# A four-layer graph network: the hidden pass's softmax inverses spread by DMA instead of matmul, and an adjacency asked for ahead

## The chip, the cores and the metric

The kernel runs on one NeuronCore of a Trainium2 chip. The metric is the device time of one execution in microseconds (us), lower is better; times are medians over runs. Five engines with instruction queues of their own share the work: PE (matmuls), DVE (vector), ACT (scalar), POOL (GpSimd) and SP, which here only issues transfers (DMAs). ACT and POOL issue transfers too. PSUM is the memory of eight banks that matmuls write into.

## The reference

Four layers on a graph of n = 3327 nodes with 256 features each. Every layer is `x = layernorm(x + gnn(x, adj))`.

```python
# layer 0: pairwise scores through all 256 features
score = einsum('ijc,c->ij', leaky_relu(g_src[:, None] + g_tgt[None]), a_w)   # masked by adj
y0 = softmax(score) @ g_tgt
# layer 1 (and 2, without leaky_relu): scores are a sum of two numbers
e = leaky_relu(s1[:, None] + s2[None, :]);  e = where(adj == 0, -1e9, e)
y1 = softmax(e) @ (h @ W.T)
# layer 3: two passes of four heads with 64 features each
h = einsum('nf,hfd->hnd', x, W)
e = leaky_relu(f1[:, :, None] + f2[:, None, :], 0.2)                          # masked by adj
out = elu(einsum('hnm,hmd->hnd', softmax(e), h))                              # heads side by side
```

Layer 3 applies its pass twice, the second time on the output of the first. In layers 1 and 3 exp(leaky_relu(a + b)) is a maximum of two products, so that one entry of the weight matrix is a `max` and a `mult` (by the adjacency). The sum over a row of weights is carried along as one more column, and the division by it comes at the end.

## The kernel before, in words

The nodes form 26 tiles of 128 rows (the last has 127). Columns of the result are worked in four **blocks** of 7, 7, 6 and 6 tiles, 896 or 768 columns wide.

Layer 0 (`sparse0`) gathers neighbours' rows by indirect DMAs on POOL. On its way it already makes layer 1's features of tiles 0 to 19 and stores them in DRAM (`feats_d`). The last six tiles are normalised and projected after layer 0, by generators that run beside layer 1's first block: `last_group` reads their sums back (`take`, DMAs of ACT), yields four times, takes the statistics (`settle`) and normalises; then `prepare` turns and projects them.

Layers 1 to 3 are in `layers`. `one_head` does layers 1 and 2, `many_heads` the two passes of layer 3 (`l3a`, `l3b`). Both loop over blocks, and within a block over the 26 tiles j of neighbours. In layer 1 `adjacent` loads the int32 adjacency tile `at_i` (SP), casts it to bf16 (`at`, ACT, L1638) and stores it to `at_d` for the later layers, which load it from there. `weigh` (L1621, DVE) makes the weights `e` from `rate`, a feature column and the adjacency. PE multiplies them with the features: L1705 in `one_head`; in `many_heads` L1752 for the features (eight groups of 32 rows, two halves of the columns) and L1760 for the sums of the weights.

`e` and `at_i` share one ring of eight buffers, the tag "e" of the pool `edges`. In layer 3 one j needs four `e` tiles, one for each head. In that ring the kernel also puts `sums`, the copy of the sums of a finished block.

The order in which the engines take up work is mostly the order in which the program is written (`manual_schedule`): on PE all through, on DVE and ACT in layer 3 and in layer 1's first block. `in_order` also holds POOL and SP to it, and is closed at the end of that block. Elsewhere a scheduler places the instructions.

Side work is done by generators in the list `pending`: `work_off` takes one step of them after the matmuls of j=0 and of every j from 4 on, one yield being one step. Thus the finishing of a block of layer 3 runs beside the next block. `finish_hidden` does that for `l3a`. It takes `inverses` (L1795: for each tile a matmul of `sums` with `heads_at` turns the sums over to partitions, and DVE takes reciprocals). Then it works on units of two tiles in stages, each so many steps after the first (`staged`, lags 0, 3, 6, 7): `spread` multiplies each inverse column, broadcast to 64 columns, with the identity (L1834), so that every partition has its row of inverses, and ACT copies the result; `scale` multiplies `o` by it and starts the elu (`below`, two ACT instructions); `elu` ends it; `project` (L1549) makes the second pass's features. `send_rates` and `load_rates` pass the second pass's rates through DRAM. `finish_last` does the same for `l3b`, with `inverses`, transposes back (L1883), the elu, the residual and the norm (`add`).

The tag "spread" of the pool `work` has four buffers, for `spreads`, `both`, `rate_rows` and others.

Of the kernel before, what the change touches and what calls it, by code (L numbers as in the profile page):

```python
# [50 lines left out]
def gat_stack(  # L51
# [59 lines left out]
    feats_d = dram.tile([EARLY * P, dim + 2], F32, name="feats_d")  # L111

# [157 lines left out]
    def sparse0(lost):  # L270
        GROUP, TURNS, LEAD, SPREAD = 4, 22, 8, 8
        starts = [sum(SETS[:s]) for s in range(len(SETS))]
        with ExitStack() as s0:
# [1028 lines left out]
            def last_group():  # L1302
                s = len(SETS) - 1
                take(s)
                for _ in range(4):
                    yield
# [191 lines left out]
    def layers(rs, early=0, rest=None):  # L1498
# [127 lines left out]

        def adjacent(j, b, first=False):
# [8 lines left out]
            at_i = edges.tile([P, wide], I32, tag="e", name="at_i", bufs=8)  # L1636
            copy_rows(nc.sync, at_i[:pn, :w], adj_t[j * P : j * P + pn, c0:c1])
# [51 lines left out]
        def one_head(layer, nxt, banks_next):  # L1689

            for b, block in enumerate(blocks):
                work_until(lambda: not layer.leaky or layer.rate[b] is not None)
                accs = [bank(s) for s in range(len(block))]
                for j in range(nt):
# [17 lines left out]
                    if layer is l1 and b == 0:  # L1712
                        work_off(2 if j > 10 else 1)
                        fetch([j + 3])
                        if j > early and late:
                            l1.load_rates(late.pop(0))
                    elif j >= LATER:
                        work_off()
# [10 lines left out]
                if b == 0:  # L1729
                    nxt = nxt()  # L1730
                pending.append(prepare(nxt, b, banks_next, normed=False))

        def many_heads(layer, nxt, finish):

            pairs = layer.nh // 2
            for b, block in enumerate(blocks):
# [34 lines left out]
                sums = edges.tile([P, wide], F32, tag="e", name="sums", bufs=8)  # L1771
# [3 lines left out]
                for x, (lo, hi) in enumerate(parts):  # L1775
                    nc.scalar.copy(sums[:, lo:hi], accs[x][pairs][:, : hi - lo])
# [12 lines left out]
        def inverses(block, sums, inv):  # L1789
# [3 lines left out]
            for s, it in enumerate(block):  # L1793
                pn = rows_of(it)
                nc.tensor.matmul(  # L1795
                    turned[:pn, s * heads : (s + 1) * heads], sums[:, s * P : s * P + pn], heads_at,
                    start=True, stop=True,
# [16 lines left out]
        def finish_hidden(b, o, sums):  # L1814
            block = blocks[b]
            inv = small.tile([P, max(sizes) * heads], F32, tag="invs", name="invs", bufs=2)
            yield from inverses(block, sums, inv)
            held = {}

            def cols(u):  # L1820
                return u[0] * P, min((u[-1] + 1) * P, cols_of(block)[1] - cols_of(block)[0])

            def spread(u):

                lo, hi = cols(u)
                m = misc((6, 7))
                m = m.rearrange("p (x i) -> p x i", x=heads // 2)
                for s in u:
                    pn = rows_of(block[s])
                    at0 = s * P - lo  # L1830
                    for h_of in range(heads):
                        p, q = divmod(h_of, 2)
                        k = s * heads + h_of
                        nc.tensor.matmul(  # L1834
# [262 lines left out]
```

## Time and profile before

| | |
|---|---|
| median of 3 runs | 2979.46 us (2978.26 to 2981.44) |
| the profiled execution's own time | 2983.31 us |
| its span in the profile | 2981.5 us |
| mean granted PE clock | 0.871 |
| busy: PE, DVE, ACT, POOL | 79%, 72%, 28%, 33% of the span |
| layer 0 | 0 to about 1363 us |
| layer 1, first block | about 1363 to 1465 us |
| `l3a` and `l3b` | about 1975 to 2981 us |

The table is read with the strip of 40 slices (each 74.5 us; a digit is the busy share in tenths): the stages have different bounds, and a share over the whole span says little about one of them. The stages' times are from the timeline. A group line of the profile has the line of the kernel, the engine, the operation, what it writes and reads, and the shapes; a line of the timeline begins with its start and its length in us, and ends with how many instructions it merges and with the idle time before them.

### The profile page before, as it was taken

The page shows a single profiled execution, that of the slowest core. Times are in us where ns is not written, and L with a number is a line of the kernel's source. Part 1 is how long each engine was busy: PE and PEld are TensorE (multiplying, and loading weights), DVE is VectorE, ACT ScalarE, POOL GpSimd, SP SyncE. Part 2 cuts the span into 40 slices and gives each one's busy share as a digit, 9 for nine tenths or more (in the row PEclk, how much of TensorE's full clock was granted, in tenths as well). Part 3 has the DMA queues.
Part 4 walks back from the last instruction along what each step waited for, and adds up shares of the span by engine and source line. Part 5 has one row for each costly group of instructions (what it writes and reads, how often), then busy time and mean ns, then how long its engine had stood idle before and what let it go on. Part 6 is the DMA issues. An engine that isn't in the chain of part 4 may idle for free.

```text
span 2981.5 us, 45479 instructions
## 1 busy us (share of the span) xinstructions
PE 2345.0 (79%) x16101; PEld 1308.0 (44%) x16122; DVE 2141.0 (72%) x5633; ACT 846.6 (28%) x2372; POOL 992.6 (33%) x1061
## 2 busy tenths in 40 slices
PE   7566757556554506557999999999999999999997
PEld 4222323222221203225888888853444554534332
DVE  6789799968876437764455421158989889899997
ACT  3244445443343304443344311101011110110111
POOL 2676767777777777770000000000000000000000
PEclk8577778777677758888999999999999999999998
DMA  7785665545544345446766533321221221212211
GB/s 234 202 262 144 186 170 161 143 134 160 156 115 110 107 112 145 132 123 188 240 199 199 164 94 106 105 85 47 69 72 44 73 66 51 69 45 62 56 46 47
DMA packets 178607, 366.95 MB, mean 123 GB/s; under 512 B 34140, under 2 KB 119467, under 8 KB 177348
## 3 DMA queue, kind: packets, MB, share of 16 engines
q1 hardware_dynamic: 103994, 178.49, 21.3%
q0 software_dynamic: 51008, 155.70, 19.2%
q10 hardware_dynamic: 23370, 29.76, 2.9%
q8 instruction: 130, 2.13, 0.3%
q14 instruction: 105, 0.86, 0.1%
HBM read 324.06 MB, written 46.12 MB: 124 GB/s over the span
## 4 chain that ended last, share of the span: by engine, by line
PE 47%; DVE 4%; DMA 2%; issue 1%; ACT 0%; POOL 0%; DVEq 0%; POOLq 0%; SPq 0%; ACTq 0%
PE acc L1752 18%; PE acc L1705 16%; PE acc L1760 9%; PE misc L1549 3%; DVE e L1621 3%; DMA at<-at_d 1%; DMA at_i<-in_adj_t_dram 1%; PE misc L1648 0%; PE misc L1834 0%; PE misc L1795 0%; DVE stats L1912 0%; DVE h L1910 0%; DVE both L1907 0%; DVE h L249 0%; DMA h<-sums_d 0%
## 5 line engine op out<-in xcount | busy, mean ns | idle before, releaser
L904 POOL DMA_INDIRECT g<-table_d,lst x894 | 851.9, 953 | 275.2 <-issue 245.7
L1621 DVE SCALAR_TENSOR_TENSOR e<-rate,feat,at 128x896 f32<-128x896 f32 (+4 forms) x832 | 844.1, 1079 | 82.0 <-PE acc L1760 69.7
L1007 PE MATMUL acc<-g,ident 128*128 128x512 f32 (+1 forms) x896 | 508.5, 712 | 263.6 <-ACT g L1004 238.9
L1752 PE MATMUL acc<-e,feat 128*32 128x384 f32 (+2 forms) x6656 | 690.4, 516 | 8.2 <-DVE h L1725 5.3
L1752 PEld LDWEIGHTS acc<-e,feat 128*32 128x32 f32 x6656 | 258.8, 110 | 348.7 <-issue 236.3
L1007 PEld LDWEIGHTS acc<-g,ident 128*128 128x128 f32 x896 | 196.4, 229 | 482.4 <-ACT g L1004 363.4
L1760 PE MATMUL acc<-e,feat 128*32 128x384 f32 (+3 forms) x3328 | 376.0, 513 | 0.0
L1004 ACT ACTIVATE g<-g,w 128x256 f32<-128x256 f32 x883 | 365.5, 495 | 0.4 <-ACT minus L481 0.4
L924 DVE TENSOR_TENSOR y<-g,minus_ps 128x1028 f32<-128x1028 f32 (+2 forms) x233 | 273.4, 1173 | 124.3 <-DMA g<-table_d,lst 112.3
L930 DVE SCALAR_TENSOR_TENSOR y<-y,a_ps 128x257 f32<-128x257 f32 x894 | 324.3, 418 | 25.7 <-PE a_ps L773 5.9
L1705 PE MATMUL acc<-feat,e 128*128 128x257 f32 (+2 forms) x1352 | 304.4, 382 | 12.0 <-DVE e L1621 8.8
L243 POOL TENSOR_TENSOR rstds<-rstds,minus_half 128x7 f32<-128x7 f32 (+1 forms) x12 | 19.7, 1641 | 774.4 <-DVE rstds L242 774.4
L1705 PEld LDWEIGHTS acc<-feat,e 128*128 128x128 f32 (+2 forms) x1352 | 255.5, 191 | 50.0 <-DVE e L1621 10.0
L1705 PE MATMUL acc<-feat,at 128*128 128x257 bf16 (+2 forms) x2028 | 239.5, 275 | 5.6 <-DMA at<-at_d 5.3
L1705 PEld LDWEIGHTS <-at 128*128 128x128 bf16 (+2 forms) x2028 | 199.5, 100 | 40.2 <-DMA at<-at_d 5.9
L1760 PEld LDWEIGHTS acc<-e,feat 128*32 128x32 f32 (+1 forms) x3328 | 139.2, 110 | 154.3 <-issue 130.7
L545 PE MATMUL v<-code,leads 65*128 65x512 bf16 (+1 forms) x182 | 83.0, 458 | 156.3 <-DVE cand L571 112.4
L1621 DVE SCALAR_TENSOR_TENSOR e<-rate,feat,at_i 128x896 f32<-128x896 f32 (+2 forms) x104 | 111.6, 1080 | 88.9 <-DMA at_i<-in_adj_t_dram 60.5
L571 DVE MAX8 cand<-v 128x8 f32<-128x104 f32 (+2 forms) x858 | 158.8, 259 | 20.8 <-PE v L548 19.9
L1601 POOL DMA_DIRECT2D rate3b_d<-rate_rows x4 | 2.1, 519 | 469.0 <-ACT rate_rows L1600 469.0
L1638 ACT CAST at<-at_i 128x896 bf16<-128x896 int32 (+2 forms) x104 | 92.0, 885 | 99.6 <-DMA at_i<-in_adj_t_dram 67.4
L545 PEld LDWEIGHTS <-leads 65*128 65x128 bf16 x182 | 22.3, 122 | 190.4 <-DVE cand L571 155.8
(249 smaller groups left out, 1873.9 us busy)
## 6 DMA issues: line engine op xcount, KB each, us to landing
adj_i<-in_adj_dram SPq DMA_DIRECT2D x75, 512.0 KB, 4.1
at<-at_d SPq DMA_DIRECT2D x150, 224.0 KB, 2.5
at_i<-in_adj_t_dram SPq DMA_DIRECT2D x50, 448.0 KB, 4.3
at<-at_d SPq DMA_DIRECT2D x75, 192.0 KB, 2.4
at<-at_d SPq DMA_DIRECT2D x75, 191.8 KB, 2.4
g<-table_d,lst POOLq DMA_INDIRECT x894, 2.8
at_d<-at ACTq DMA_DIRECT2D x50, 224.0 KB, 4.2
at_i<-in_adj_t_dram SPq DMA_DIRECT2D x25, 384.0 KB, 3.5
```

The costliest lines, as they stand in the source:

```text
L545: nc.tensor.matmul(v[:, :w], leads[:, b, :], code[:, :w], start=True, stop=False)
L571: nc.vector.max(spread[:, c0 + c, :], view(v[:, :w]))
L904: nc.gpsimd.indirect_dma_start(out=g[:, k - k0, :], out_offset=None, in_=table_d[:, :], in_offset=bass.IndirectOffsetOnAxis(ap=entry["lst" ...
L924: nc.vector.tensor_tensor(y, rows, minus_src[:, None, :].to_broadcast([P, m, dim + 1]), op=ALU.max)
L930: nc.vector.scalar_tensor_tensor(y, y, 1.0, a_ps[:, : dim + 1], op0=ALU.mult, op1=ALU.mult, accum_out=sc)
L1004: nc.scalar.activation(rows, rows, AF.Copy, scale=w[:, k : k + 1])
L1007: nc.tensor.matmul(dst, ident, rows, start=start, stop=stop)
L1621: nc.vector.scalar_tensor_tensor(e[:pn, : c1 - c0], self.rate[b][:pn, h_of, : c1 - c0], q, at[:pn, : c1 - c0], op0=ALU.max, op1=ALU.mult,)
L1638: nc.scalar.copy(at[:pn, :w], at_i[:pn, :w])
L1705: nc.tensor.matmul(accs[s][:pn, : dim + 1], a[:pj, s * P : s * P + pn], f[:pj, : dim + 1], start=(j == 0 and part == 0), stop=(j == nt - 1 ...
L1752: nc.tensor.matmul(accs[x][p][q : q + 32, : hi - lo], f[:pj, at0 : at0 + 32], es[at0 // hd][:pj, lo:hi], start=(j == 0), stop=(j == nt - 1),)
L1760: nc.tensor.matmul(accs[x][pairs][h_of * 32 : (h_of + 1) * 32, : hi - lo], f[:pj, dim + h_of : dim + h_of + 1].to_broadcast([pj, 32]), es[ ...
```

## The change

In `finish_hidden` the inverses are no longer made and spread by matmuls. The sums (one row per head, in two tiles of the tag "spread" instead of one of the ring "e") go to DRAM, come back as 128 partitions of 28 columns (24 in the blocks of six tiles), DVE takes the reciprocals at once, they go to DRAM again, and for each unit two DMAs read them, broadcast over 64 partitions each. All of these DMAs are issued by ACT. The stages' lags become 0, 2, 4, 5. `finish_last` keeps `inverses`, with the sums read from the two new tiles.

In layer 1's first block, `ask` requests the adjacency three tiles ahead, the first three before the loop and before the loads of the first features. SP's order of the program is kept until after layer 2's set-up (`sp_order`), so that layer 2's loads come after the block's adjacency tiles. `last_group` yields six times instead of four.

```diff
+    sums3_d, inv3_d = [
+        [
+            dram.tile([heads, (nt // 4 + (b < nt % 4)) * P], F32, name=f"{what}3{b}_d")
+            for b in range(4)
+        ]
+        for what in ("sums", "inv")
+    ]
...
                 take(s)
-                for _ in range(4):
+                for _ in range(6):
                     yield
                 yield from settle(s)
...
+        asked = {}
+
+        def ask(j, b):
+
+            pn = rows_of(j)
+            c0, c1 = cols_of(blocks[b])
+            at_i = asked[j, b] = edges.tile([P, wide], I32, tag="e", name="at_i", bufs=8)
+            copy_rows(nc.sync, at_i[:pn, : c1 - c0], adj_t[j * P : j * P + pn, c0:c1])
+
         def adjacent(j, b, first=False):
...
-            at_i = edges.tile([P, wide], I32, tag="e", name="at_i", bufs=8)
-            copy_rows(nc.sync, at_i[:pn, :w], adj_t[j * P : j * P + pn, c0:c1])
+            if (j, b) not in asked:
+                ask(j, b)
+            at_i = asked.pop((j, b))
...
                     if layer is l1 and b == 0:
                         work_off(2 if j > 10 else 1)
+                        if j + 3 < nt:
+                            ask(j + 3, b)
                         fetch([j + 3])
...
                 if b == 0:
                     nxt = nxt()
+                    sp_order.close()
...
-                sums = edges.tile([P, wide], F32, tag="e", name="sums", bufs=8)
+                sums = [
+                    work.tile([P, BANK], F32, tag="spread", name="sums", bufs=4) for _ in parts
+                ]
+                if c1 - c0 < len(block) * P:
+                    lo, hi = parts[-1]
+                    nc.vector.memset(sums[-1][:, hi - lo : len(block) * P - lo], 1.0)
...
-                    nc.scalar.copy(sums[:, lo:hi], accs[x][pairs][:, : hi - lo])
+                    nc.scalar.copy(sums[x][:, : hi - lo], accs[x][pairs][:, : hi - lo])
...
         def finish_hidden(b, o, sums):
             block = blocks[b]
+            total = cols_of(block)[1] - cols_of(block)[0]
+            width, half = len(block) * P, (len(block) + 1) // 2 * P
+            few = heads * width // P
             inv = small.tile([P, max(sizes) * heads], F32, tag="invs", name="invs", bufs=2)
-            yield from inverses(block, sums, inv)
             held = {}
 
+            for x, t in enumerate(sums):
+                lo, hi = x * half, min((x + 1) * half, width)
+                nc.scalar.dma_start(
+                    sums3_d[b][:, lo:hi],
+                    t.rearrange("(h r) i -> h r i", h=heads)[:, 0, : hi - lo],
+                )
+            yield
+            yield
+            nc.scalar.dma_start(
+                inv[:, :few], sums3_d[b].rearrange("h (a c) -> (h a) c", c=few)
+            )
+            yield
+            nc.vector.reciprocal(inv[:, :few], inv[:, :few])
+            yield
+            nc.scalar.dma_start(
+                inv3_d[b].rearrange("h (a c) -> (h a) c", c=few), inv[:, :few]
+            )
+            yield
+            rows = inv3_d[b].rearrange("(p q) i -> q p i", q=2)
...
             def spread(u):
 
                 lo, hi = cols(u)
-                m = misc((6, 7))
-                m = m.rearrange("p (x i) -> p x i", x=heads // 2)
-                for s in u:
-                    pn = rows_of(block[s])
-                    at0 = s * P - lo
-                    for h_of in range(heads):
-                        p, q = divmod(h_of, 2)
-                        k = s * heads + h_of
-                        nc.tensor.matmul(
-                            m[q * hd : (q + 1) * hd, p, at0 : at0 + pn],
-                            inv[:pn, k : k + 1].to_broadcast([pn, hd]),
-                            ident[:pn, :pn], start=True, stop=True,
-                        )
                 t = held[u[0]] = work.tile(
                     [P, heads // 2, 2 * P], F32, tag="spread", name="spreads", bufs=4
                 )
-                nc.scalar.copy(t[:, :, : hi - lo], m[:, :, : hi - lo])
+                for q in range(2):
+                    nc.scalar.dma_start(
+                        t[q * hd : (q + 1) * hd, :, : hi - lo],
+                        rows[q : q + 1, :, lo:hi].to_broadcast([hd, heads // 2, hi - lo]),
+                    )
...
-            yield from staged(units, [(0, spread), (3, scale), (6, elu), (7, project)])
+            yield from staged(units, [(0, spread), (2, scale), (4, elu), (5, project)])
...
+        sp_order = ExitStack()
+        sp_order.enter_context(tc.manual_schedule(engines={mybir.EngineType.SP}))
         in_order = ExitStack()
         in_order.enter_context(
             tc.manual_schedule(
                 engines={
                     mybir.EngineType.DVE, mybir.EngineType.Activation, mybir.EngineType.Pool,
-                    mybir.EngineType.SP,
                 }
             )
         )
...
             l1.load_rates(late.pop(0), nc.sync)
+        for j in range(3):
+            ask(j, 0)
         fetch(range(3))
```

## The prediction

> **What bounds the kernel now.** I read the strip of 40 slices first, then the chain, then the timeline of the two stages that the change touches.
>
> ```profile
> PE   7566757556554506557999999999999999999997
> DVE  6789799968876437764455421158989889899997
> ...
> PE acc L1752 18%; PE acc L1705 16%; PE acc L1760 9%; PE misc L1549 3%; DVE e L1621 3%; DMA at<-at_d 1%; DMA at_i<-in_adj_t_dram 1%; PE misc L1648 0%; PE misc L1834 0%; PE misc L1795 0%; DVE stats L1912 0%; DVE h L1910 0%; DVE both L1907 0%; DVE h L249 0%; DMA h<-sums_d 0%
> ```
>
> From slice 19 on (about 1400 us) PE is at 9 throughout, and the chain runs through its matmuls. DVE stands at 8 or 9 in layer 3 (from 1975 us). So in layer 3 a microsecond of PE work is a microsecond of time, as long as DVE keeps up. The PE timeline shows what the side work costs:
>
> ```profile
> 2131.76 3.19 PE L1752 MATMUL acc<-e,feat 128*32 128x512 f32 x32
> 2134.77 1.69 PE L1760 MATMUL acc<-e,feat 128*32 128x512 f32 x16
> 2136.27 3.19 PE L1752 MATMUL acc<-e,feat 128*32 128x512 f32 x32
> 2139.28 1.69 PE L1760 MATMUL acc<-e,feat 128*32 128x512 f32 x16
> 2140.90 1.09 PE L1834 MATMUL misc<-ident,invs 128*64 128x128 f32 x16
> 2141.92 3.21 PE L1752 MATMUL acc<-e,feat 128*32 128x512 f32 x32
> ```
>
> A plain j iteration takes 4.51 us (2131.76 to 2136.27), one with a `spread` 5.65. With 768 columns the pair is 3.87 and 5.00. PE never idles between them. A second line is the DVE timeline where a block of layer 3 begins:
>
> ```profile
> 2724.64 2.88 DVE L1621 SCALAR_TENSOR_TENSOR e<-rate,feat,at 128x768 f32<-128x768 f32 x3 [0.19 <-PE acc L1760]
> 2729.16 8.67 DVE L1621 SCALAR_TENSOR_TENSOR e<-rate,feat,at 128x768 f32<-128x768 f32 x9 [1.64 <-PE acc L1760]
> ```
>
> Three `e` tiles of the new block are made, the fourth waits 1.64 us until the last matmul of the old block is over: `sums` took one of the eight `e` buffers. Layer 1's beginning is the one place after layer 0 where PE stands idle for long:
>
> ```profile
> 1363.07 3.27 PE L1705 MATMUL acc<-feat,e 128*128 128x257 f32 x14 [1.14 <-issue]
> 1372.66 4.97 PE L1705 MATMUL acc<-feat,e 128*128 128x257 f32 x14 [6.32 <-DVE e L1621]
> 1379.42 3.30 PE L1705 MATMUL acc<-feat,e 128*128 128x257 f32 x14 [1.79 <-DVE e L1621]
> 1384.35 1.97 PE L1705 MATMUL acc<-feat,e 128*128 128x257 f32 x8 [1.63 <-issue]
> ...
> 1367.00 0.32 SPq L1982 DMA_DIRECT2D feat<-feats_d  x1
> 1367.36 0.43 SPq L127 DMA_DIRECT2D at_i<-in_adj_t_dram  x1
> ```
>
> j=0 runs, then j=1 waits for `e`, which waits for an `at_i` that SP asks for only at 1367.36, behind a `feat` load that cannot go before 1367.00, when layer 0's buffers are free.
>
> **What the Trainium skill says.** "Perfetto Trace Analysis", Identifying Performance Opportunities: the same gap repeating on the saturated engine can mean that a buffer is missing. The trace agrees: 0.7 to 0.9 us at each of the seven block changes of layer 3. "DMA: Bandwidth & Descriptors", Anatomy of one DMA: about 2.0 us fixed per transfer, mostly completion, and a wait is taken on the issuing sequencer. The trace agrees: 128 KB `out_dram` lands after 2.4 us in layer 3; and ACT, which will issue the new transfers, will stand at their waits. "TensorE: Matmul & The Clock Gate", What's actually happening: after an idle window PE restarts at a lower clock. The trace fits: j=1, after 6.32 us idle, takes 4.97 us where the others take 3.3.
>
> **Part by part.**
>
> *Spread matmuls removed* (28 or 24 per finished block of `l3a`, two records each). Excess of the iterations that hold them: block 1 3 x 1.13 + 0.70 = 4.1; block 2 the same, 4.1; block 3 3 x 1.13 = 3.4; first block of `l3b` 3.4. Together -15.0 us. The 14 copies on ACT go as well, at no gain: ACT is busy 13% there.
>
> *Inverses by matmul removed in `l3a`, `sums` out of the ring.* In block 1 the last iteration of block 0 starts at 2106.67 and the second of block 1 at 2118.21: 11.54, that is 2 x 4.51 + 2.52. The same reading gives 2.60, 2.37 and 2.29 at the next three changes; sum -9.8. Of it 1.73 or 1.50 each (14 or 12 records of L1795) is the matmul, the other 0.8 the missing buffer. The three later changes in `l3b` keep their matmuls and lose the buffer wait: 0.77 + 0.92 + 0.72 = -2.4. The `spread` buffers that `sums` takes instead were freed many iterations before.
>
> *What DVE then bears.* `e` for one iteration takes 4.24 us of PE's 4.51 (896 columns), 3.70 of 3.87 (768). In the `add` steps of `l3b`, DVE ends its four tiles 1.43 us after PE starts on them (2661.94 against 2660.51) and PE loses 0.70 per iteration, so the slack is 0.73; for 768 I take 0.52. `scale` and `elu` cost 0.60 each (L1847 starts at 2150.91, the next `e` at 2151.51). Before they fell in different iterations, with PE's spread between; now lags 2 and 4 put two of them into one, 1.2 us, while PE's projection (2.1 us) comes an iteration later. Followed step by step, PE waits about 0.3 us in each 896 block and 0.9 in each 768 block: +2.4 us. From both sides: 0, if more is banked, to 7, if each of the ten double steps costs 0.7.
>
> *Transfers added:* 12 DMAs per 7-tile block on ACT's queue (two `sums`, one read, one write, eight spreads), 10 per 6-tile block, about 0.35 us of issue each as for `at_d`, on an idle queue. Nothing else of the block stands behind them but `below` and the features of the same finish. `sums` goes out at j=0 and is wanted by DVE's reciprocal at j=6, over 20 us later; the reciprocal at j=6 and the first `scale` at j=10 leave 15 us for one write and one read. The tight one is the second unit: its spread is issued behind `below` of the first (0.64 + 0.63 on ACT), then 0.7 of issue; the next `scale` comes two iterations later, 9.0 or 7.7 us after the first. So 6.9 or 5.6 us remain for landing; I take 2.5 us, the nearest row. The new traffic (under 1.5 MB per block) lies on DMA engines busy 22%, against `at` loads asked for up to three iterations ahead: nothing. The memset of `sums`, 0.07 us, is done while PE works.
>
> *Layer 1.* In the new SP order the first four `at_i` stand among layer 0's last stores, so they have landed by 1200; `e` for j=0 and j=1 is made there. The `feat` loads 0 to 2 then stand behind one more `feats_d` store, so DVE's wait before its first `e` (13.57 us, 1177.31 to 1190.87) may grow by some 3 us. POOL's gathers set the time there, they go on at 0.3 us idle each to 1343, and DVE has caught up by 1205: nothing. After 1363.07 j=0 to 2 run through to about 1372.2. j=3 needs `feat` 3, asked for at 1367.00 and landed some 4 us later: `e` at about 1372. j=3 starts near 1372.5 instead of 1384.35. Next late are the buffers that ACT's casts free behind its seven `h<-sums_d` issues (1368.41 to 1375.38) and the `at_i` after them; I allow 3 us. Gain 9; both sides: 1 (those waits hold all) and 12.4 (the 11.7 and the 0.73 of idle at 1451). The `l2w` and `l3aw` loads leave this queue's start and come before the block's end, where four `e` tiles lie ahead of PE: nothing. The two more yields of `last_group` put two more `e` ahead of its norms; features 20 to 25 are still made by j=16, before j=20.
>
> **Sum:** -15.0 - 9.8 - 2.4 + 2.4 - 9 = -33.8 us. The profiled run took 2983.31 (span 2981.5), 3.9 above the median 2979.46; so 2949.5 there, and 2945.6 as a median: **2946 us**.
>
> **Rivals.**
>
> *The transfers come late (slower).* DVE would stand at `scale` with all its `e` behind it, and PE would follow. Ten units wait on a spread issued behind the one before. At a landing of 13 us each stall is 5.4 (896) or 6.9 us (768), five of each, 61 in all, less 21 that PE's ten projections give back: 40 lost, net +6: 2986. It decides from about 12 us. For it: 64 partitions read the same kilobytes; a broadcast of `rate` landed in 9.7 us in layer 1. Against: in layer 3 broadcasts of 14 times the size land in 7.5. Chance 0.06.
>
> *DVE becomes the bound in `l3a`.* It has 0.17 us per iteration to spare at 896 and less at 768. If the ten double steps cost 1 us more each: 2956. For it: `l3b`'s iterations of 5.18 and 5.71 show just this. Against: PE's projection gives back 2.1 each time. Chance 0.12.
>
> *Asking ahead moves the wait only.* `h<-sums_d` (5.94 us in the chain just before an `at_i`) and the features hold j=3 to 6 as now: gain 1 of 9, 2954. Chance 0.16.
>
> The likeliest has 0.66. A difference of 0.2% (6 us) is about what can be told from no change here. The range joins the parts' ends without the first rival, gains of 20 to 40 us, and the 1.5 us by which the runs before differ: 2938 to 2961. Faster 0.92, within 0.2% 0.02, slower 0.06.
>
> **What would show it.** Right: no L1834 records; iterations of 4.51 and 3.87 except at projections; no wait of the fourth `e` at a block's start; L1705 running on from 1363 to about 1372. Wrong: DVE waiting for `spreads` or the reciprocal, iterations above 4.51 at the double steps by more than 1 us, or j=3 of layer 1 near 1380.

## The result, and the profile after

The changed kernel takes 2955.03 us (median of 6 runs, 2953.0 to 2958.08), the kernel before 2980.45 us in the same set (6 runs, 2975.32 to 2985.57): a ratio of 0.9911, with a 95% interval of 0.9900 to 0.9921. The forecast was 2946 us, so of 33.8 us of gain some 25 came. In a later set of runs the change took 2954.60 us against 2979.81, a ratio of 0.9915 (0.9903 to 0.9928). The profiled execution of after has its own time of 2953.03 us and a span of 2951.3; before had 2983.31 and 2981.5.

In the first two groups of experiments below, layer 0 took 420 to 455 us longer in every kernel (the kernel before takes 3400 and 3422 us in all there), while the layers after it kept their times to a few microseconds; the experiments are therefore compared from layer 1's first matmul on.

The page of the changed kernel ("after") first: the strip of 40 slices (tenths of busy time) and the chain that ended last, by line.

```profile
PE   7466657556545416657899999999999999999997
...
DVE  6789789968776527765445521138999999899997
...
PE acc L1773 18%; PE acc L1723 16%; PE acc L1781 9%; DVE e L1629 3%; PE misc L1557 3%; DMA at<-at_d 1%; PE misc L1666 0%; DMA at_d<-at 0%; DMA at_i<-in_adj_t_dram 0%; DVE stats L1952 0%; DVE h L1950 0%; DVE h L1745 0%; DVE both L1947 0%; PE misc L1822 0%; DVE h L257 0%
```

The picture is the one of before: PE is still the bound from slice 19 on. The spread matmuls are gone from the chain (L1834 of before has no successor). L1773 and L1781 are the main matmuls that were L1752 and L1760; L1723 is layer 1's, L1705 before; L1629 is `e`, L1621 before.

PE's timeline in layer 3, in block 1 where a `spread` stood before:

```profile
2126.60 3.36 PE L1773 MATMUL acc<-e,feat 128*32 128x512 f32 x32
2129.61 1.85 PE L1781 MATMUL acc<-e,feat 128*32 128x512 f32 x16
2131.11 3.36 PE L1773 MATMUL acc<-e,feat 128*32 128x512 f32 x32
```

From 2126.60 to 2131.11 is the plain iteration of 4.51 us, and there is no longer one of 5.65 us. DVE's timeline where a block of 768 columns begins in `l3a`:

```profile
2225.25 3.81 DVE L1629 SCALAR_TENSOR_TENSOR e<-rate,feat,at 128x768 f32<-128x768 f32 x4 [0.17 <-PE acc L1781]
...
2229.76 10.62 DVE L1629 SCALAR_TENSOR_TENSOR e<-rate,feat,at 128x768 f32<-128x768 f32 x11 [0.71 <-PE acc L1781]
```

Four tiles of the new block are now made ahead, not three. PE's timeline at layer 1's beginning, and then at the start of its second block:

```profile
1363.54 15.40 PE L1723 MATMUL acc<-feat,e 128*128 128x257 f32 x70 [1.14 <-issue]
1379.27 18.47 PE L1723 MATMUL acc<-feat,e 128*128 128x257 f32 x84 [0.33 <-DVE e L1629]
...
1461.38 2.05 PE L1723 MATMUL acc<-feat,e 128*128 128x257 f32 x4 [4.93 <-DVE inv L1744]
```

At 14 matmuls to an iteration the first line is j=0 to 4 without a gap; j=5 waits 0.33 us where j=1 of before waited 6.32. The last line is new: PE stands 4.93 us at the block's end, which before had no gap. After the gap the matmuls are slower too: four take 2.05 us there, where the block's last seven had taken 1.68. The granted PE clock is 1.00 from 1446 to 1456 us, 0.50 from 1461.4 to 1463.4 and again from 1463.8 to 1465.8, and 1.00 from 1467 to 1477. DVE's timeline shows what PE waits for:

```profile
1455.78 1.15 DVE L1629 SCALAR_TENSOR_TENSOR e<-rate,feat,at_i 128x896 f32<-128x896 f32 x1 [2.33 <-DMA at_i<-in_adj_t_dram]
1456.85 0.76 DVE L164 TENSOR_TENSOR dots<-l3aw,dst 128x256 f32<-128x256 f32 x2
...
1459.17 1.14 DVE L1629 SCALAR_TENSOR_TENSOR e<-rate,feat,at_i 128x896 f32<-128x896 f32 x1
...
1460.56 0.16 DVE L1744 RECIPROCAL inv<-acc 128x1 f32<-128x1 f32 x1
```

PE had finished the block at 1456.45. The evacuation of its accumulators (L1744 and L1745, which empty PSUM for the next block) stands on DVE behind dot products of layer 3's weights and behind `e` tiles of the next block, one of which had waited for its adjacency. From 1456.45 to 1460.56 DVE itself is hardly idle: most of this stretch is the dot products with their sums and one `e`.

The starts of the iterations (of the first matmul of each) in the two profiles, subtracted, give where the 30 us between the two spans come from:

| part | forecast | measured in the profiles |
|---|---|---|
| spread matmuls | -15.0 | 4.18 + 4.19 + 3.45 + 3.47 = -15.3 |
| inverses and buffer, changes of `l3a` | -9.8 | 2.55 + 2.62 + 2.39 + 2.32 = -9.9 |
| three later changes of `l3b` | -2.4 | 0.58 + 0.07 + 0.07 = -0.7 |
| DVE's operations closer together | +2.4 | 0.45 + 1.1 + 1.1 + 0.45 = +3.1 |
| transfers | 0 | 0 |
| layers 1 and 2, with layer 0's end | -9 | -7.1 |
| sum | -33.8 | -29.9 (span -30.2) |

### The profile page after: what moved, and what is told of

It reads as the page before. It is cut to its first block, busy times and chain, and to the rows that moved or that the text cites. A ratio compares the mean times of both kernels' runs of the same rounds, so it can differ in the third digit from the quotient of the medians.

```text
span 2951.3 us, 45054 instructions
## 1 busy us (share of the span) xinstructions
PE 2329.5 (79%) x15841; PEld 1364.5 (46%) x15862; DVE 2140.5 (73%) x5634; ACT 840.2 (28%) x2358; POOL 991.6 (34%) x1061
## 4 chain that ended last, share of the span: by engine, by line
PE 46%; DVE 5%; DMA 2%; issue 1%; ACT 0%; DVEq 0%; SPq 0%; ACTq 0%; POOL 0%; POOLq 0%
PE acc L1773 18%; PE acc L1723 16%; PE acc L1781 9%; DVE e L1629 3%; PE misc L1557 3%; DMA at<-at_d 1%; PE misc L1666 0%; DMA at_d<-at 0%; DMA at_i<-in_adj_t_dram 0%; DVE stats L1952 0%; DVE h L1950 0%; DVE h L1745 0%; DVE both L1947 0%; PE misc L1822 0%; DVE h L257 0%
## 5 line engine op out<-in xcount | busy, mean ns | idle before, releaser
L1629 DVE SCALAR_TENSOR_TENSOR e<-rate,feat,at 128x896 f32<-128x896 f32 (+4 forms) x832 | 843.4, 1080 | 58.6 <-PE acc L1781 47.2
L1015 PE MATMUL acc<-g,ident 128*128 128x512 f32 (+1 forms) x896 | 516.4, 721 | 257.3 <-ACT g L1012 232.5
L1773 PE MATMUL acc<-e,feat 128*32 128x384 f32 (+2 forms) x6656 | 697.4, 515 | 7.2 <-DVE h L1745 4.2
L1773 PEld LDWEIGHTS acc<-e,feat 128*32 128x32 f32 x6656 | 307.1, 110 | 305.3 <-issue 159.1
L1781 PE MATMUL acc<-e,feat 128*32 128x384 f32 (+3 forms) x3328 | 383.3, 512 | 0.0
L1723 PE MATMUL acc<-feat,e 128*128 128x257 f32 (+2 forms) x1352 | 303.9, 382 | 7.4 <-DVE inv L1744 4.9
L1723 PEld LDWEIGHTS acc<-feat,e 128*128 128x128 f32 (+2 forms) x1352 | 255.2, 191 | 45.3 <-issue 7.8
L1723 PE MATMUL acc<-feat,at 128*128 128x257 bf16 (+2 forms) x2028 | 237.8, 274 | 4.6 <-DMA at<-at_d 4.4
L1781 PEld LDWEIGHTS acc<-e,feat 128*32 128x32 f32 (+1 forms) x3328 | 162.1, 110 | 130.7 <-issue 88.1
L1723 PEld LDWEIGHTS <-at 128*128 128x128 bf16 (+2 forms) x2028 | 198.8, 99 | 38.3 <-DMA at<-at_d 4.9
L1629 DVE SCALAR_TENSOR_TENSOR e<-rate,feat,at_i 128x896 f32<-128x896 f32 (+2 forms) x104 | 112.3, 1081 | 91.5 <-DMA at_i<-in_adj_t_dram 47.0
```

The costliest lines, as they stand in the source:

```text
L1015: nc.tensor.matmul(dst, ident, rows, start=start, stop=stop)
L1629: nc.vector.scalar_tensor_tensor(e[:pn, : c1 - c0], self.rate[b][:pn, h_of, : c1 - c0], q, at[:pn, : c1 - c0], op0=ALU.max, op1=ALU.mult,)
L1723: nc.tensor.matmul(accs[s][:pn, : dim + 1], a[:pj, s * P : s * P + pn], f[:pj, : dim + 1], start=(j == 0 and part == 0), stop=(j == nt - 1 ...
L1773: nc.tensor.matmul(accs[x][p][q : q + 32, : hi - lo], f[:pj, at0 : at0 + 32], es[at0 // hd][:pj, lo:hi], start=(j == 0), stop=(j == nt - 1),)
L1781: nc.tensor.matmul(accs[x][pairs][h_of * 32 : (h_of + 1) * 32, : hi - lo], f[:pj, dim + h_of : dim + h_of + 1].to_broadcast([pj, 32]), es[ ...
```

## Experiments

In the table are the times, in us, of one profiled execution of each: from layer 1's first matmul to the first of its second block, to the first of layer 3, layer 3 itself to PE's last instruction, and the whole from layer 1 on.

| kernel | first block | layers 1 and 2 | layer 3 | from layer 1 on |
|---|---|---|---|---|
| before | 104.3 | 612.5 | 988.9 | 1601.4 |
| the change | 97.9 | 604.9 | 965.8 | 1570.7 |
| change_again | 98.7 | 605.7 | 965.7 | 1571.4 |
| before_sums | 105.1 | 611.7 | 984.5 | 1596.2 |
| old_lags | 98.1 | 606.7 | 964.6 | 1571.3 |
| early_weights | 105.2 | 611.7 | 965.4 | 1577.1 |
| order_closed_early | 99.6 | 605.6 | 965.4 | 1571.0 |
| evacuation_first | 92.6 | 599.7 | 965.4 | 1565.0 |
| lags_2_3_4 | 98.7 | 605.6 | 987.7 | 1593.4 |
| lags_1_2_3 | 98.7 | 609.6 | 987.8 | 1597.4 |
| one_step | 91.4 | 599.1 | 965.4 | 1564.5 |
| second_unit_later | 99.4 | 609.3 | 972.8 | 1582.2 |
| evacuation_and_one_step | 86.5 | 593.3 | 965.4 | 1558.6 |
| all_three | 87.2 | 595.7 | 973.0 | 1568.7 |

Layer 3 repeats within 0.5 us where it is not touched. Layer 2, which no edit touches, took 266.4 to 271.5 us from its first matmul to layer 3's first, with its waits for `at<-at_d`; differences of up to 5 us in the second column can be chance (604.9 to 609.6 us in the six kernels whose layer 1 is the change's). Layer 1 alone tells more: 337.2 to 339.1 us in these six.

**change_again**: nothing is edited; the change ran once more beside the last three kernels below.

> The change itself once more, beside the three others. Its layers 1 to 3 should take the 1570.7 us of the first profile within 3 us, whatever layer 0 takes; the kernel before took 1601.4, so the difference should stay at 30 us and the time be 25 to 30 us below the kernel before.

It came as expected: 1571.4 us from layer 1 on, 25.2 us below before in the medians.

### What the buffer is worth

**before_sums**: the kernel before with the sums out of the ring and nothing else (`inverses` reads the two new tiles).

```diff
-                sums = edges.tile([P, wide], F32, tag="e", name="sums", bufs=8)
+                sums = [
+                    work.tile([P, BANK], F32, tag="spread", name="sums", bufs=4) for _ in parts
+                ]
...
-                    nc.scalar.copy(sums[:, lo:hi], accs[x][pairs][:, : hi - lo])
+                    nc.scalar.copy(sums[x][:, : hi - lo], accs[x][pairs][:, : hi - lo])
...
```

> The kernel before with one part of the change alone: the sums go into two spread buffers instead of one of the eight e buffers; inverses and spreads still by matmul. Theory of the prediction (the missing e buffer costs PE about 0.8 us at each of the seven block changes of layer 3): the seven changes become shorter by 0.8, 0.8, 0.7, 0.7, 0.77, 0.92 and 0.72 us, 5.6 us in all. Rival (those 0.8 us are the idle time of 0.62 us that PE's weight loads show ahead of every group of side matmuls, whose weights are 64 or 128 columns wide where those of the main matmuls are 32; it stays as long as the inverses are made by matmul): under 1 us in all, nearly all of it at the change into the second block of l3b, where the changed kernel already showed 0.58. The changed kernel, in which l3b keeps its matmuls and has the buffer, gained only 0.58 + 0.07 + 0.07 at its three changes, so I expect the rival to hold: time 0 to 1 us below before.

The seven changes became shorter by 0.58, 0.66, 0.66, 0.58, 0.58, 0.07 and 0.07 us, 3.2 in all (the rest of layer 3's 4.4 us lies in its first and last blocks). The medians can't show this: 3400.43 us against 3400.27, a ratio of 0.9999 (0.9982 to 1.0016), an interval some 6 us wide on either side. DVE's timeline at the change into the third block of `l3a`, first of before, then of this kernel:

```profile
2243.18 8.67 DVE L1621 SCALAR_TENSOR_TENSOR e<-rate,feat,at 128x768 f32<-128x768 f32 x9 [1.61 <-PE acc L1760]
```

```profile
2664.69 7.68 DVE L1621 SCALAR_TENSOR_TENSOR e<-rate,feat,at 128x768 f32<-128x768 f32 x8 [0.70 <-PE acc L1760]
```

With the buffer back DVE waits 0.9 us less for the old block's last matmul and makes one tile fewer after it, and PE gains 0.66. So the rival of this experiment, which I had expected to hold, falls at the first five changes: the buffer is worth 0.6 us there. It follows too what the inverses cost: 2.52 - 0.58 = 1.94 us for 14 records of 1.73 us together.

At the last two changes the buffer is worth 0.07 us, although their excess had looked alike: 0.66 and 0.46 us are left over the plain iteration and the inverses' 1.94 and 1.71. PE's timeline shows what these are, first at the change above in before_sums, then at the last but one change in the changed kernel (127 rows are the old block's last tile, 128 the new block's first):

```profile
2662.80 1.85 PE L1760 MATMUL acc<-e,feat 127*32 127x512 f32 x16
2664.30 2.93 PE L1752 MATMUL acc<-e,feat 128*32 128x384 f32 x32
```

```profile
2699.22 0.50 PE L1773 MATMUL acc<-e,feat 128*32 128x384 f32 x2
2699.42 0.49 PE L1781 MATMUL acc<-e,feat 127*32 127x384 f32 x2
2699.55 0.49 PE L1773 MATMUL acc<-e,feat 128*32 128x384 f32 x2
2699.74 0.49 PE L1781 MATMUL acc<-e,feat 127*32 127x384 f32 x2
```

At the last two changes the iterations overlap: the new block's first matmul starts 0.53 and 0.32 us before the old block's last, where at the other five it starts 0.13 after it. An iteration counted from its first matmul is then longer by 0.66 and 0.45 us without any loss: from the old block's last matmul to the first inverse it is 4.28 or 4.29 us in before_sums at all four changes into a block of 768 columns, the last two included (in before 4.94 twice, then 4.36 and 4.35). Why the late `e` costs PE only 0.07 us at the last two is not shown.

### What the double steps cost

**old_lags**: the change with the lags of before.

```diff
-            yield from staged(units, [(0, spread), (2, scale), (4, elu), (5, project)])
+            yield from staged(units, [(0, spread), (3, scale), (6, elu), (7, project)])
```

> The changed kernel with the lags of the kernel before (scale 3 steps, elu 6 and projection 7 steps after the spread, instead of 2, 4 and 5), so that scale and elu fall in different iterations. Theory (DVE's two operations of 0.69 us in one iteration make it late once in each block): the iteration of the first projection becomes as long as the others that hold a projection, 6.60 instead of 7.06 us in the blocks of 896 columns and 5.96 instead of 7.06 in those of 768, so layer 3 is 0.45 + 1.10 + 1.10 + 0.45 = 3.1 us shorter, and the time some 3 us below that of the change. Rival (the late e is due to the projection itself, or to the transfers): the excess moves with the projection and the time is that of the change.

It took back 0.26 + 0.15 + 0.15 + 0.25 = 0.8 us and not 3.1. So it isn't that two operations meet in one iteration. DVE's timeline of the change in block 1:

```profile
2149.28 0.69 DVE L1887 TENSOR_TENSOR o<-o,spreads 128x512 f32<-128x512 f32 x1
2149.89 8.59 DVE L1629 SCALAR_TENSOR_TENSOR e<-rate,feat,at 128x896 f32<-128x896 f32 x8
2158.39 0.68 DVE L1893 SCALAR_TENSOR_TENSOR o<-spreads,o 128x512 f32<-128x512 f32 x1
2158.99 0.69 DVE L1887 TENSOR_TENSOR o<-o,spreads 128x512 f32<-128x512 f32 x1
```

DVE runs without a break: `e` of two iterations takes 8.5 us of PE's 9.02, and three operations of 0.6 us each fall ahead of the first projection (PE at 2167.76), with either set of lags. The theory of a debt: DVE falls behind PE by the time of these operations less the slack of the iterations between, and PE waits once for what is left. The old lags have one iteration more between, whose slack, PE's 4.51 or 3.87 us less the 4.24 or 3.70 of `e`, is 0.27 or 0.17; that fits the 0.26 and 0.15 us.

**lags_2_3_4** and **lags_1_2_3** bring the projection nearer, so that only two operations precede it; the second also tests how near the transfers are to being late.

```diff
-            yield from staged(units, [(0, spread), (2, scale), (4, elu), (5, project)])
+            yield from staged(units, [(0, spread), (2, scale), (3, elu), (4, project)])
```

> The changed kernel with elu 3 and projection 4 steps after the spread instead of 4 and 5. The old lags (3, 6, 7), in which no two DVE operations fall in one iteration, took back only 0.30 + 0.15 + 0.15 + 0.25 us of the 3.1 that the first projections lose. So the theory now is a debt: DVE bears three operations of 0.69 us before the first projection gives it PE's 2.1 us, whatever the iterations they fall in; here it is two (scale, elu). Debt theory: the first projection's iteration falls from 7.06 to about 6.6 (896 columns) and to 6.3 (768), 0.45 + 0.7 + 0.7 + 0.45 = 2.3 us less in layer 3. Rival (a fixed cost of the first projection, such as o or the bank coming late): 7.06 as before, no gain.

```diff
-            yield from staged(units, [(0, spread), (2, scale), (4, elu), (5, project)])
+            yield from staged(units, [(0, spread), (1, scale), (2, elu), (3, project)])
```

> The changed kernel with lags 1, 2 and 3: the scale comes one iteration after its spread was issued, 4.51 or 3.87 us. It measures how near the transfers were to being late. The prediction assumed a landing of 2.5 us: then DVE waits nowhere for spreads, and with one operation before the first projection less than in the change layer 3 is about 2.3 us shorter, as with 2, 3, 4. Rival (the broadcasts take several times that, as the one of rate took 8.5 us in layer 1): DVE waits at the first and later scales for spreads, by the landing less 3.9 to 4.5 us each; at a landing of 6 us, some 2 us in each of 14 units, layer 3 is 10 to 20 us longer.

Both lost 22 us in layer 3 against the change, nearly its whole gain of 23 there. The waits ahead of `elu` (L1893) in lags_2_3_4, us and times, and one of them in DVE's timeline:

```profile
  ACT spreads L1839: 37.0, 10
```

```profile
2622.29 0.69 DVE L1893 SCALAR_TENSOR_TENSOR o<-spreads,o 128x512 f32<-128x512 f32 x1 [3.73 <-ACT spreads L1839]
```

Ten `elu` wait 3.7 us each for ACT's two passes of `below`. With these lags `project` of one unit and `scale` of the next fall in one step, so `below` stands on ACT behind the features of the projection, which wait for PE; the `elu` one step later waits with them, and every `e` behind it. In the change two steps lie between `scale` and `elu`. Neither theory had this, and the runs tell nothing of the debt. They do tell of the transfers: in lags_1_2_3, where a scale follows its spread by one iteration, no scale waited for `spreads`, though the nearest started 3.74 us after the end of its issue.

**second_unit_later** is the cleaner test of the debt: lags 2, 4, 5, but all units after the first one step later.

```diff
-                (tuple(range(s, min(s + 2, len(block)))), s) for s in range(0, len(block), 2)
+                (tuple(range(s, min(s + 2, len(block)))), s + (s > 0)) for s in range(0, len(block), 2)
```

> The changed kernel with the units after the first begun one step later in the finish of l3a (at steps 0, 3, 5, 7 instead of 0, 2, 4, 6); the lags stay 2, 4, 5, so that no elu comes nearer to ACT's work on a projection than in the change (with lags 2, 3, 4 DVE stood 3.7 us at ten elu for ACT, which was behind a projection's features). Debt theory: DVE bears two operations of 0.69 us ahead of the first projection instead of three; the first projection's iteration falls from 7.06 us to 6.6 (896 columns) and to about 6.4 (768), 0.45 + 0.6 + 0.6 + 0.45 = 2.1 us less in layer 3 (965.4 us). Rival (a fixed cost of the first projection): 7.06 stays and layer 3 is the same.

The first projection's iteration did fall, by 0.29, 0.61, 0.60 and 0.28 us: 1.8 of the 2.1 expected, which supports the debt. But layer 3 became 7 us longer. The waits ahead of `scale` (L1887) in this kernel, then lines of ACT's and of DVE's timeline around one of them:

```profile
  DMA spreads<-inv_d: 12.6, 4
```

```profile
2174.65 0.17 ACT L1566 ACTIVATE feat<-misc 128x4 f32<-128x4 f32 x1 [17.36 <-PE misc L1557]
...
2177.49 1.24 ACTq L1879 DMA_DIRECT2D spreads<-inv_d  x2
```

```profile
2181.84 0.69 DVE L1887 TENSOR_TENSOR o<-o,spreads 128x512 f32<-128x512 f32 x1 [2.83 <-DMA spreads<-inv_d]
```

Here a spread falls in the step of a projection. ACT waits for PE until 2174.65, works on the features until 2176.8, starts `below`, and only then issues the two halves, until 2178.73; DVE goes on at 2181.84. This is what the forecast's slower rival feared, with another cause: not that a transfer takes long (3.11, 3.96, 2.96 and 3.29 us from the end of its issue to DVE's start in the four cases), but that its issue is late, behind ACT's work on the features. The four waits are 2.83, 3.85, 2.85 and 3.02 us.

### Where layer 1's gain went

Asking ahead won 11.2 us by j=5; at the second block's j=1 only 3.7 were left. The first theory was that the weights of layers 2 and 3a, now loaded at the block's end, hold DVE up there.

**early_weights** loads them, and makes their dot products, at j=12.

```diff
                     if layer is l1 and b == 0:
+                        if j == 12:
+                            nxt = nxt()
                         work_off(2 if j > 10 else 1)
...
                 if b == 0:
-                    nxt = nxt()
+                    if layer is not l1:
+                        nxt = nxt()
                     sp_order.close()
```

(`second` makes layer 3a there as well.)

> The changed kernel with the weights of layers 2 and 3a loaded, and their dot products made on DVE, at j=12 of layer 1's first block instead of at its end. Theory (at the end of that block DVE's evacuation of the accumulators stands behind dot products that wait for rows loaded only there, so PE is idle 4.93 us and the next iteration is 2.3 us longer; this takes back 7.4 of the 11.1 us that asking ahead had won): the gap at the block's end shrinks below 1 us, and layer 2 begins 4 to 7 us earlier than in the changed kernel; time 4 to 7 us below the change. Rival (DVE is late there because the adjacency tiles land late, with or without the weights): the gap stays at 2 us or more and the gain is under 2.5 us. A second rival: DVE waits for the rows at j=12 so long that PE runs out of e there; then a new gap shows near 1410 us.

The second rival came at j=12 to 14: DVE waited 4.83 and 4.65 us for rows, PE ran out of `e` for 4.24 us, and the block took 7.4 us longer than in the change. And the gap at the block's end was still 4.71 us, with no dot product near it.

**order_closed_early** ends SP's written order where it ended before.

```diff
                 in_order.close()
+                sp_order.close()
...
                     nxt = nxt()
-                    sp_order.close()
```

> The changed kernel with SP's written order ended where it ended before, ahead of layer 1's evacuation, so that the scheduler places the loads of the weights of layers 2 and 3a: it puts l2w and l3aw among the first features again and the rows ahead of the block's last adjacency tiles. If the lateness of those loads is what the longer order cost, the gap of 4.93 us at the end of layer 1's first block becomes 0 to 2 us, while j=1 to 3 lose 0.5 to 2 us to the two loads that stand in front of the features again: 3 to 6 us less than the change in all. If the adjacency is what DVE lacks, the gap stays.

The gap was 5.82 us. So the theory of the weights falls: in the change the dot products fill part of the stretch, but where they are gone waits for the adjacency fill it instead. DVE's timeline of this kernel at the block's end:

```profile
1875.69 1.15 DVE L1629 SCALAR_TENSOR_TENSOR e<-rate,feat,at_i 128x896 f32<-128x896 f32 x1 [2.17 <-DMA at_i<-in_adj_t_dram]
1878.11 1.15 DVE L1629 SCALAR_TENSOR_TENSOR e<-rate,feat,at_i 128x896 f32<-128x896 f32 x1 [1.27 <-DMA at_i<-in_adj_t_dram]
1881.36 1.15 DVE L1629 SCALAR_TENSOR_TENSOR e<-rate,feat,at_i 128x896 f32<-128x896 f32 x1 [2.10 <-DMA at_i<-in_adj_t_dram]
1882.43 0.29 DVE L1745 RECIPROCAL inv<-acc 128x1 f32<-128x1 f32 x3
```

PE had finished at 1877.4. Three `e` tiles of the next block stand ahead of the evacuation on DVE, where the scheduler places the instructions from here on, and each waits for an adjacency tile. "Perfetto Trace Analysis" of the Trainium skill, Tensor Engine Instruction (MATMUL, LD_WEIGHTS), says that DVE takes its instructions in strict order, unlike PE; the trace agrees, since the reciprocal, whose input is ready at 1877.4, starts at 1882.43.

**evacuation_first** writes the order out: two `e` of the next block, then the evacuation, and layer 2's weights three iterations later.

```diff
-                in_order.close()
+                if layer is l1 and b == 0:
+                    for x in range(2):
+                        ahead[x, 1] = layer.weigh(x, 1, adjacent(x, 1, True), 0)
                 for s, it in enumerate(block):
...
+                    if layer is l1 and (j, b) == (3, 1):
+                        in_order.close()
+                        nxt = nxt()
+                        sp_order.close()
+                        pending.append(prepare(nxt, 0, banks_next, normed=False))
```

> The changed kernel with the evacuation of layer 1's first block written out on DVE behind two e tiles of the next block, and the weights of layer 2 asked for three iterations later. In the runs so far the gap at that block's end stayed at 4.7 to 5.8 us wherever the weights were loaded, and DVE stood ahead of the evacuation at two or three e tiles of the next block whose at_i had not landed. Theory (the evacuation queues on DVE behind those e): the gap falls from 4.93 us to about 1 us; DVE is then 7 us with the evacuation and its statistics, so the third e comes some 1.7 us late; from layer 1's start to layer 3's start 3 to 5 us less than the change (604.9 us). Rival (the adjacency itself is what is short: 448 KB in and 224 KB out per 3.03 us, at a DMA share of 0.9 there): PE stands later in the same block for what it did not stand at its start, and the stage is within 1.5 us of the change.

PE's timeline there:

```profile
1875.71 21.01 PE L1727 MATMUL acc<-feat,e 128*128 128x257 f32 x96
1896.89 0.67 PE L1727 MATMUL acc<-feat,e 128*128 128x257 f32 x2 [0.18 <-DVE mvs L243]
```

The gap is gone but for waits of 0.18 us, and layer 1 takes 331.7 us, 5.5 less than in the change; layer 3 begins 5.2 us earlier. The next block's first iteration still takes 5.16 us (5.66 in the change, 3.03 for a plain one), for another reason: the granted clock is 1.00 throughout, and PE goes at the pace of the evacuation, two matmuls for each tile that DVE empties, every 0.85 us. PE does not stand later for what it did not stand here. The edit moves the weights as well, but two other places for them had left the gap.

**one_step** takes the side work of the first block one step per iteration.

```diff
-                for _ in range(6):
+                for _ in range(4):
...
-                        work_off(2 if j > 10 else 1)
+                        work_off()
```

> The changed kernel with layer 1's side work taken one step per iteration throughout (and four empty steps ahead of it as before the change), instead of two per iteration from j=11. In the change six iterations of 5.18 us hold a turn and a projection each, 2.15 us over 3.03, in which PE stands 0.83 us for ACT; one step at a time costs 0.22 and 0.88 over 3.03 (the kernel before at j=8 and 9). So PE's own work up to j=21 becomes 6 us shorter. Theory (the adjacency's transfers limit the end of this block): PE then waits for e at j=18 to 25, and the block's end comes at most 2 us earlier. Rival (PE and ACT set it): from layer 1's start to the next block 5 to 6 us less than the 97.85 us of the change.

The rival holds: 6.4 us less in the first block. Most of this is not the gain that got lost, since the kernel before takes two steps per iteration from j=11 as well; it is a further gain. PE's timeline of the change with two steps per iteration, and of this kernel with one:

```profile
1400.83 1.04 PE L1557 MATMUL misc<-w,turned 128*128 128x258 f32 x4
1402.69 0.44 PE L1666 MATMUL misc<-ident,h 128*128 128x128 f32 x2 [0.83 <-ACT columns L1584]
1402.97 3.20 PE L1723 MATMUL acc<-feat,e 128*128 128x257 f32 x14
```

```profile
1839.72 3.20 PE L1723 MATMUL acc<-feat,e 128*128 128x257 f32 x14
1842.75 0.38 PE L1666 MATMUL misc<-ident,h 128*128 128x128 f32 x2
1842.97 3.20 PE L1723 MATMUL acc<-feat,e 128*128 128x257 f32 x14
1846.01 1.03 PE L1557 MATMUL misc<-w,turned 128*128 128x258 f32 x4
```

In one iteration the turn after a projection waits 0.83 us for ACT, which is at the features; an iteration apart, main matmuls lie between and nothing waits. The adjacency, with a DMA share of 0.9 near the block's end, was not the limit. The gap at the block's end stays (the last iteration takes 7.72 us).

**evacuation_and_one_step** and **all_three** put the edits together.

> Both edits of layer 1 together. Alone they brought 5.2 us (599.65 us from layer 1's start to layer 3's) and 6.4 us (599.1), by different places: the gap at the end of the first block, and the pairs of side steps from j=11 to j=16. If what they take away is independent, 593 us, and 2936 to 2945 us where the change takes 2955. If the adjacency's transfers are near their limit (a DMA share of 0.9 to 1.0 at the block's end), the second adds less than 3 us: 596 us or more.

> Both edits of layer 1 and the later second unit: if they add, from layer 1's start to the end 1556 us where the change has 1570.7 (593 + 963.3), some 14 us below the change in the same runs.

The two edits of layer 1 add: 593.3 us, as expected, and 325.9 for layer 1 alone. This kernel takes 2943.36 us (4 runs, 2938.36 to 2947.3), a ratio to before of 0.9881 (0.9865 to 0.9896), 11 us below the change in the same runs, and is the fastest here. With the later second unit added it takes 2948.73 us, for the reason shown above.

## Why the forecast was right, and where it was not

*The spreads and the inverses* (24.8 us forecast, 25.2 measured): right, since both were read as excess of whole iterations on a saturated PE. The inner split was a little off: 0.8 us was given to the buffer in each of these four changes, and before_sums measures 0.58 to 0.66.

*The later changes of `l3b`* (2.4 forecast, 0.7 measured): the mis-sized term. The step that failed is reading the excess over plain iteration and inverses as the wait for the fourth `e`. DVE's wait of 1.64 us at 2729.16, the one that the prediction shows, is real, but with the buffer back that change is only 0.07 us shorter: 0.66 us of its excess, and 0.45 at the last change, is the overlap of two iterations. So the trace bears out the missing buffer at five of the seven changes, not at all seven.

*DVE* (+2.4 forecast, +3.1 measured): the size was near, the reason half wrong, so the near size is in part luck. "Two of them in one iteration" is not what costs; what counts, as far as old_lags and second_unit_later go, is how many operations DVE bears before the first projection. The lags of before would have cost about 2.3 us of it too, which the kernel before did not show: its first projections take 6.62 and 5.99 us there. Its spread matmuls, 1.13 us each on PE, were time for DVE as well; that this is what covered the debt is argued, not tried.

*Transfers* (nothing): right. Their landing was taken as 2.5 us and takes 3.0 to 4.0, and the issue of two takes 1.24 us, not 0.7. In the changed kernel every scale starts at least 5.1 us after the end of its issue, so 1 to 2 us are left at the tightest. The section that the prediction cites for 2.0 us describes transfers issued by GpSimd; these are issued by ACT. What decides is ACT's order: one step of displacement brought waits of 2.8 to 3.9 us.

*Layer 1* (-9 forecast): the first half came as told. L1723 runs on from 1363.54, j=3 starts at 1372.71, and DVE's wait in layer 0 did not hold it up (12.80 us and then 0.96, against 13.56). The later waits, allowed for with 3 us, came to 0.6, so that 11.1 us were won up to the block's last iteration. The step that failed is "before the block's end, where four `e` tiles lie ahead of PE: nothing". I looked at the loads as a delay of `e` and not at what DVE has to do at that point: the evacuation, which PE needs at once and which is queued behind them. It gave back 5.1 us at the block's end and 2.3 in the next iteration. Of the latter only 0.38 is a wait for DVE; the rest falls under the granted clock of 0.50 after the gap, where matmuls start 0.43 us apart instead of 0.22. The prediction had this cost in its own lines, in the j=1 of 4.97 us after 6.32 us of idle time. The third rival, that asking ahead only moves the wait, had thus a real part, in another place than it named. The two more empty steps, costed at nothing, turned two iterations with a single step into one more double one, and 1.05 us were lost by it between j=8 and j=18, by the iteration starts. Of the measured 7.1 us some 3.7 lie in layer 2, which the change does not touch and which varies by as much; layer 1 itself gave the other 3.4. That the sum of this part lies near its forecast is luck.

*The median.* The sum was off by 3.5 us in the profiled execution. The other 6 us come from carrying over the 3.9 us by which the profiled run of before stood above its median; the changed kernel's profiled run stands 2.0 below its own.

## What to carry to other kernels

On a saturated engine, side work read as the excess of whole iterations was priced here within a few tenths of a microsecond; a share of that excess put down to a wait on another engine is only a guess until the wait is taken away, and where iterations overlap, part of an excess is no time at all. When work is moved to an in-order queue, ask for each urgent instruction (an evacuation, the issue of a transfer) what stands ahead of it and what that waits for: here an evacuation behind prefetched tiles cost 5 us and some 2 more at a halved clock after the gap, and a transfer's issue behind a projection's features 3 us each time. And for an engine with little slack, count the operations that it bears before its next relief; how they fall mattered less here.

## What was not expected of the hardware

PE's weight loads show 0.62 us of idle time ahead of the groups of side matmuls in layer 3 whose weights are 64 or 128 columns wide, among main matmuls of 32, for instance ahead of the projection at 2167.76. It looks like a cost of the switch, but 14 inverses cost 1.94 us in all where their records show 1.73: at most 0.2 us of the 0.62 is lost time.

Layer 0's 894 indirect gathers on POOL, by group, in before and in before_sums (busy us, mean ns | idle before):

```profile
L904 POOL DMA_INDIRECT g<-table_d,lst x894 | 851.9, 953 | 275.2 <-issue 245.7 <-PE acc L1007 12.4 <-DMA g<-table_d,lst 7.1
```

```profile
L904 POOL DMA_INDIRECT g<-table_d,lst x894 | 851.7, 953 | 389.0 <-issue 285.0 <-PE acc L1007 68.0 <-remote 24.8
```

The same code takes the same time per gather and stands 114 us longer before them, with layer 0 423 us longer (1786.6 against 1363.1 us to layer 1's first matmul). The two groups with the long layer 0 ran on two other chips than the last group, where it took its usual time; whether the chip is the cause, no run here tells. After layer 0 the stages agree to a few microseconds.
